# Five small moves in the order of a one-core transformer block: row loads, zeros, turned pair rows, a weight load and late sums

## The chip, the core and the metric

The kernel runs on one core of one Trainium2 chip. The metric is the device time of one execution in microseconds. The core has a matrix engine (TensorE, "PE", with its weight loads "PEld"), VectorE ("DVE"), ScalarE ("ACT"), GpSimd ("POOL") and SyncE ("SP"), which run side by side and wait for each other by semaphores. Each executes its own instructions in order. Transfers (DMAs) are issued by SP, ACT and POOL.

## What is computed

Eight sequences (batches) of 512 rows of 256 numbers go through an attention layer and a mixture of experts, each normalized before and after and added to its input:

```python
x = L0_attn_x
x = x + _layernorm(_L0_attn_ref(_layernorm(x, axis=-1), ...), axis=-1)
x = x + _layernorm(_L0_ffn_ref(_layernorm(x, axis=-1), ...), axis=-1)
```

The attention has 16 query heads of 128 over 4 groups of keys and values, with sinusoidal positions added to queries and keys, and is causal:

```python
scores = jnp.einsum('bgqtd,bgksd->bgqts', q, k) / math.sqrt(D)
scores = jnp.where(causal, scores, -jnp.inf)
probs = jax.nn.softmax(scores, axis=-1)
out = jnp.einsum('bgqts,bgksd->btgqd', probs, v).reshape(b, t, G * QPG * D)
return out @ wo
```

The second layer sends each row to the best 6 of 64 experts by a softmax over gate scores. An expert takes at most 64 rows, the first in the order of rows; what it takes more of counts as zero. A shared expert is added for all rows:

```python
g = jax.nn.silu(jnp.einsum('ech,ehf->ecf', buf, w_gate))
u = jnp.einsum('ech,ehf->ecf', buf, w_up)
d = jnp.einsum('ecf,efh->ech', g * u, w_down)
...
y = y + gs * us @ sh_down.T
```

## The kernel before

**Steps.** The main loop (lines 998 to 1061) runs over 128 steps, one for each head of each batch: step k is head s = k mod 16 of batch b = k // 16. A step holds the scores of head k (`scores`, L328: four blocks of rows `psc`, 0 to 3, each reduced by VectorE with the mask, L332, and put through the exponential by ScalarE, L335), the weighting of the last results (`weigh`: a reciprocal on VectorE, L342, and four multiplications on POOL, L345), the output projection of head k-3 (`project`, L402), the queries of head k+1 (`queries`, L315 and L318) and the product of probabilities and values of head k-2 (`mix`, L390). The order of instructions on all engines is written by hand: what stands first in the Python program stands first in each engine's queue.

**Turned blocks.** For `mix` the probabilities must be transposed. `turned` does so for head k-1 in step k, between the scores of rows 1 and 2: VectorE transposes 32x32 blocks into `eb` (L361), SP writes them to DRAM in four pieces (`ex_d`, L366) and reads them back in the other order as `et` (L371). Rows of a batch that are needed transposed take the same way (`exchange_rows`): four writes to `exr_d` (L133), and a read (L135) that waits in a list and is issued by the next `turned` between its writes and its read of `et`. In this way the next batch's normalized rows become `xr_a`, and the rows of the second layer become `xt2` ("xt" in the profile) for batches 0 to 3.

**Work beside the heads.** `side(s, place)` calls what is planned for a place of a step: A after `weigh`, B after `project`, M after `queries`, D after `mix`. There the second layer of batch b-1 runs in the steps of batch b (`feed_forward`): sums, norms and residuals, the turn of its rows (6M), the shared expert (psg and psu of L749 from step 8 for batches 0 to 3, whose steps from 7 on stand one later, else from 7), the routing, and for batches up to 4 the store of rows and scores into a table in DRAM. `prepare(b+1)` is the other side chain: it loads the next x (L167, called in step 6 before `queries`), takes its norms at the end of step 7 (L78, `st_a`), turns its rows in step 9 and makes keys and values. x has two buffers. `zeros` (L228) writes zeros into the second half of `y_d`, in 21 pieces of 128x256 after a first call; in batch 0 each step asks for two of them, after `mix` (L1034).

**Expert pairs.** The rows of batches 0 to 4 (EARLY = 5) go through 32 pairs of experts (`experts`, L662). One advance of this generator is half of a pair's turn m. In the first half stand the gather of pair m's rows by POOL (`start_pair`, gx, three buffers), then `down` of pair m-5 (pd, L616), `gate_up` of m-3 (pgu, L590), `turn_hidden` of m-4 (pth, L607, and the copy ht), `turn_rows` of m-2 (two transposes ptx, L579, VectorE's copy gxt and the copy gw of two columns, L583), and the weight loads of pairs m-1 (wgu) and m-3 (wd), issued by ACT. In the second half stand `gate_up_hidden` of m-3 (two VectorE instructions, L599 and L600) and the scattering sum by POOL (`scatter`, L627) of m-5. From step 98 on a step has four slots: after the scores of rows 1, after `project`, after `mix` and at its end; first halves fall on the second and fourth, second halves on the first and third. psc, ptx and pth all take their PSUM buffers in turn from `ps_s`, which has three.

**The late pair.** Rows of batches 5 to 7 that still find room in an expert go through one pair, "late", whose number is computed. At step FIRST_FREE = 102, SP loads its weights (`load_gate_up` with 704 KB and `load_down` with 352 KB, L1044 and L1045); they are first used at steps 107 and 109. The next x, for batch 7, is loaded at the end of the same step.

**Early outputs.** After the last pair (step 115) two slots a step, after `queries` and at the end, serve `finish_early` (L969), which finishes batches 0 to 4 (`finish`, L699, and `output`, L686). Each batch begins four slots after the one before it: ACT loads its two halves of y from `y_d` (L703), SP its residual rows x1 one slot later (L716); VectorE adds the halves one slot later (L707); then come the sums for the norm (L78, with POOL's power, L88), and in the next slot `shifts` on VectorE (L94), the scaling on ACT (L98) and the sum with x1 on POOL (L694); two slots later SP stores. `output` also serves batches 5 and 6.

```python
            for _ in range((0, 0, 0, 0, 0, 0, 1, 0, 1, 1, 2, 1, 1, 1, 2, 1)[s] if b == EARLY + 1 else 0 if b > EARLY else
                           (0, 0, 0, 0, 0, 0, 0, 1, 0, 0, 1, 1, 2, 1, 2, 2)[s]):
                next(ahead)()
```

These lines give the places of the rest of `prepare`.

Of the kernel before, what the change touches and what calls it, by code (L numbers as in the profile page):

```python
# [11 lines left out]
F32 = mybir.dt.float32  # L12
# [4 lines left out]
ALU = mybir.AluOpType  # L17
AX = mybir.AxisListType

P = 128  # L20
B, T, E = 8, 512, 256
NT = B * T
NI = T // P
# [5 lines left out]
NH = G * QPG  # L29
NX, F, TOPK, CAP = 64, 176, 6, 64  # L30
FC = F // 2
NM = NX // 2
# [7 lines left out]
EARLY = 5  # L40
# [4 lines left out]
def sandwich_kernel(ctx, tc, x, wq, bq_t, wkv, bk_t, bv, wo, gate_wt, w_gate, w_up, w_down,  # L45
                    sh_gate_t, sh_up_t, sh_down_t, pe_t, out):
    nc = tc.nc
# [4 lines left out]
    small = ctx.enter_context(tc.tile_pool(name="small", bufs=4))  # L52
# [20 lines left out]
    def norm_scales(tiles, name):  # L73

        n = len(tiles)
        st = small.tile([P, n, 6], F32, tag="st", name=f"st_{name}")
        for i in range(n):
            nc.vector.bn_stats(st[:, i, :], tiles[i])  # L78
        return scales_of(st, n, name)
# [11 lines left out]
    def shifts(mv, rs, name):  # L91

        shift = small.tile([P, NI], F32, tag="shift", name=f"shift_{name}")
        nc.vector.scalar_tensor_tensor(shift, mv[:, :, 0], -1.0, rs, ALU.mult, ALU.mult)  # L94
        return shift
# [4 lines left out]
    def tiles_of(t):  # L100
        return [t[:, i, :] for i in range(NI)]
# [44 lines left out]
    with ExitStack() as part:  # L146
# [411 lines left out]
        def load_gate_up(key):  # L558
            l, queue = pairs[key], nc.sync if key == "late" else nc.scalar
            m = l["m"]  # L560

            l["wgu"] = p3.tile([P, 2, 2, 2, F], F32, name=f"wgu_{key}", **l.get("wgu_at", {"tag": "wgu"}))
            for k, w in enumerate((w_gate, w_up)):
                queue.dma_start(out=l["wgu"][:, :, k, :, :].rearrange("p e c f -> p e (c f)"),
                                in_=w[ds(m * 2, 2)].rearrange("e (p c) f -> p e (c f)", p=P))

        def load_down(key):
            l, queue = pairs[key], nc.sync if key == "late" else nc.scalar
            m = l["m"]
            l["wd"] = p3.tile([FC, 2, 2, E], F32, name=f"wd_{key}", **l.get("wd_at", {"tag": "wd"}))  # L570
            queue.dma_start(out=l["wd"].rearrange("p e c h -> p e (c h)"),
                            in_=w_down[ds(m * 2, 2)].rearrange("e (p c) h -> p e (c h)", p=FC))
# [53 lines left out]
        def scatter(m):  # L626
            nc.gpsimd.indirect_dma_start(  # L627
                out=y_d[:, :], out_offset=bass.IndirectOffsetOnAxis(ap=table["idx"][:, m, 1:2], axis=0),
                in_=pairs.pop(m)["dd"], in_offset=None, compute_op=ALU.add)
# [32 lines left out]
        def experts():  # L662


            yield from tables()
            yield
            later = free_slots()
            for m in range(NM + 5):
                if m < NM:
                    start_pair(m)  # L670
                for behind_, step in ((5, down), (3, gate_up), (4, turn_hidden), (2, turn_rows),
                                      (1, load_gate_up), (3, load_down)):
                    if 0 <= m - behind_ < NM:
                        step(m - behind_)
                yield
                if 0 <= m - 3 < NM:
                    gate_up_hidden(m - 3)
                if 0 <= m - 5 < NM:
                    scatter(m - 5)
                if m >= 2:  # L680
                    next(later, None)
                if m == NM + 4:
                    pairs["all"] = True
                yield

        def output(b, y, x1):  # L686

            mv, rs = norm_scales(tiles_of(y), f"y{b}")
            yield
            shift = shifts(mv, rs, f"y{b}")  # L690
            for i in range(NI):
                scale_on_act(y[:, i, :], y[:, i, :], rs, shift, i)
            for i in range(NI):
                nc.gpsimd.tensor_add(x1[:, i, :], x1[:, i, :], y[:, i, :])  # L694
            yield
            nc.sync.dma_start(out=rows_of(out, b * T), in_=x1)
            yield

        def finish(b, tags):  # L699

            ys = [q.tile([P, NI, E], F32, tag=tag, name=f"y{n}_{b}") for n, (q, tag) in enumerate(tags[:2])]
            for k in range(2):
                nc.scalar.dma_start(out=ys[k], in_=rows_of(y_d, k * (ET_ROWS + CAP) + b * T))  # L703
            yield
            x1 = residual(b, *tags[2])
            yield
            nc.vector.tensor_add(ys[0], ys[0], ys[1])  # L707
            yield
            for n, _ in enumerate(output(b, ys[0], x1)):
                yield  # L710
                if n == 1:
                    yield

        def residual(b, q, tag):
            x1 = q.tile([P, NI, E], F32, tag=tag, name=f"x1_{b}")
            nc.sync.dma_start(out=x1, in_=rows_of(x1_d, b * T))  # L716
            return x1
# [251 lines left out]
        def finish_early():  # L969
            rows = [finish(b, EARLY_TAGS + [[(p1, "xn"), (p2, "xnt")][b % 2]]) for b in range(EARLY)]  # L970
            yield

            for t in range(4 * EARLY + 3):
                for b in range(EARLY):
                    if 0 <= t - 4 * b < 7:
                        next(rows[b])
                yield

# [8 lines left out]
        behind, ahead = {}, iter(())  # L987
        routed, zeroing = experts(), zeros()
        twice, finishing = False, False
        FIRST_FREE = (EARLY + 1) * NH + 6  # L990

        def side(s, place):
            behind.pop(f"{s}{place}", lambda: None)()
            if not b:
                for u in rest.get(f"{s}{place}", ()):
                    u()

        for k in range(NK):
            b, s = divmod(k, NH)
            active = k >= EARLY * NH + 14  # L1000
            scores(k, 0)
            scores(k, 1)
            if 0 <= k - 1 < NK - 2:
                turned(k - 1)
            if twice and not finishing:
                next(routed, None)
            scores(k, 2)
            scores(k, 3)
            if k == NK - 1:
                turned_at_once(k - 1)  # L1010
            weigh(k)
            side(s, "A")
            if k >= 3:
                project(k - 3)
            side(s, "B")
            if active and not finishing:
                next(routed, None)
            if s == 9 and b <= EARLY + 1:
                next(ahead)()
            if s == 6 and b <= EARLY:  # L1020
                ahead = prepare(b + 1)
                next(ahead)()
            if k + 1 < NK:
                queries(k + 1)
            if finishing:
                next(routed, None)
            side(s, "M")
            if b <= EARLY and s == 8:
                next(ahead)()
            if k >= 2:  # L1030
                mix(k - 2)
            if active and not finishing:
                next(routed, None)
            if not b:  # L1034
                next(zeroing, None)
                next(zeroing, None)
            if k == FIRST_FREE:

                work = table["work"]
                table["rest"] = nc.values_load(work[0:1, 0:1], min_val=0, max_val=NM - 1)  # L1040
                table["m"] = nc.values_load(work[0:1, 1:2], (ET.DVE, ET.SP), min_val=0, max_val=NM - 1)
                pairs["late"] = {"m": table["m"], "wgu_at": {"tag": "wgu_late", "bufs": 1},
                                 "wd_at": {"tag": "wd_late", "bufs": 1}}
                load_gate_up("late")  # L1044
                load_down("late")  # L1045
            if s == 2 and b:
                behind = feed_forward(b - 1)
            side(s, "D")
            if s == 6 and b == EARLY + 1:
                ahead = prepare(b + 1)  # L1050
# [4 lines that stand above are left out]
            twice = active and k > EARLY * NH + NH  # L1055
            if twice and not finishing:
                next(routed, None)
            if finishing:
                next(routed, None)
            if active and not finishing and "all" in pairs:  # L1060
                routed, finishing = finish_early(), True
# [11 lines left out]
        with tc.For_i(0, table["rest"], 1) as n:  # L1073
            m = nc.values_load(table["work"][0:1, ds(n + 2, 1)], (ET.DVE, ET.SP), min_val=0, max_val=NM - 1)
# [77 lines left out]
```

## Time and profile before

| | |
|---|---|
| median of three runs | 1431.27 us (1430.13 to 1436.82) |
| the profiled execution | 1429.28 us, of which the span is 1427.6 us |
| granted TensorE clock over the span | 0.994 |
| transfers | 262.50 MB, 184 GB/s in the mean |
| VectorE, ScalarE, GpSimd busy | 895.4, 500.2 and 433.7 us |

The profile is of one execution. In a row of groups stand the line, the engine, the operation with what it writes and reads, the count, the busy time with the mean of one instruction in ns, and after the last bar the idle time before them with what ended it. A plain step takes 7.76 us of TensorE. The costliest groups around the change are these:

```profile
L345 POOL TENSOR_SCALAR e<-e,recip 128x128 f32<-128x128 f32 x508 | 268.5, 574 | 757.6 <-DVE recip L342 744.0
L361 DVE STREAM_TRANSPOSE eb<-e 128x128 f32<-128x128 f32 x756 | 227.4, 364 | 3.5 <-DMA ex_d<-eb 3.2
L627 POOL DMA_INDIRECT y_d<-dd,idx x32 | 50.9, 1591 | 102.0 <-DMA y_d<-dd,idx 51.5
```

The transfers by the line that issues them:

```profile
ex_d<-eb SPq DMA_DIRECT2D x504, 160.0 KB
et<-ex_d SPq DMA_DIRECT2D x126, 640.0 KB
wgu<-in_w_gate ACTq DMA_DIRECT2D x32, 352.0 KB
wgu<-in_w_up ACTq DMA_DIRECT2D x32, 352.0 KB
wd<-in_w_down ACTq DMA_DIRECT2D x32, 352.0 KB
y<-y_d ACTq DMA_DIRECT2D x10, 512.0 KB
x<-in_x SPq DMA_DIRECT2D x8, 512.0 KB
```

### The profile page before, as it was taken

Reading aid. Unit: us, or ns where it says so; the run is one execution under the profiler, and the core shown is the slowest. Engines: PE = TensorE matmul, PEld = TensorE weight load, DVE = VectorE, ACT = ScalarE, POOL = GpSimd, SP = SyncE. Lnnn points to the kernel's source line nnn. Section 1 sums busy time; section 2 is a strip of 40 time slices with the busy share of each in tenths; the row PEclk is TensorE's granted clock in tenths of the full one; section 3 lists DMA queues with packets and bytes.
Section 4 is the critical chain, followed back from the end, with each engine's and each line's share of the span. In section 5 each row is a group of like instructions: output and inputs, shape, how many; then the busy total and the mean of one; then the engine's idle time right before and its main releaser. Section 6 shows DMA issues by size and latency. Waiting matters only on the chain.

```text
span 1427.6 us, 18526 instructions
## 1 busy us (share of the span) xinstructions
PE 1383.4 (97%) x5230; PEld 841.4 (59%) x5230; DVE 895.4 (63%) x3127; ACT 500.2 (35%) x1432; POOL 433.7 (30%) x698
## 2 busy tenths in 40 slices
PE   9999999999999999999999999999989999999895
PEld 5665665666556665656556665655546565556463
DVE  5565577656775577557765677566656545677634
ACT  2332344224332334234422433233433333444421
POOL 2222242213321242114221232124545344444311
PEclk9999999999999999999999999999999999999998
DMA  7774566546763576455654566459999889877702
GB/s 243 204 225 146 140 181 198 146 119 171 215 177 107 150 208 193 110 140 164 207 164 125 155 173 193 107 147 276 302 246 258 225 239 252 210 236 250 240 30 82
DMA packets 167990, 262.50 MB, mean 184 GB/s; under 512 B 17212, under 2 KB 142109, under 8 KB 167885
## 3 DMA queue, kind: packets, MB, share of 16 engines
q1 hardware_dynamic: 133069, 212.00, 50.5%
q10 hardware_dynamic: 28672, 39.85, 9.4%
q0 software_dynamic: 6144, 9.44, 3.4%
q8 instruction: 42, 0.69, 0.2%
q14 instruction: 63, 0.52, 0.1%
HBM read 148.25 MB, written 112.99 MB: 183 GB/s over the span
## 4 chain that ended last, share of the span: by engine, by line
PE 80%; DMA 7%; DVE 7%; issue 2%; ACT 2%; POOL 1%; SPq 1%; ACTq 0%; DVEq 0%; POOLq 0%
PE pav L390 16%; PE psc L328 15%; PE pq L315 13%; PE po L402 13%; PE pk L285 4%; PE pv L296 4%; PE psg L749 3%; PE psu L749 3%; PE pgu L590 2%; PE py L776 2%; PE pd L616 2%; DMA wd<-in_w_down 2%; DVE eb L361 1%; DMA exr_d<-xb_f 1%; ACT e L335 1%
## 5 line engine op out<-in xcount | busy, mean ns | idle before, releaser
L345 POOL TENSOR_SCALAR e<-e,recip 128x128 f32<-128x128 f32 x508 | 268.5, 574 | 757.6 <-DVE recip L342 744.0
L335 ACT ACTIVATE e<-e,least 128x128 f32<-128x128 f32 (+3 forms) x512 | 285.8, 559 | 349.2 <-DVE least L332 337.1
L328 PE MATMUL psc<-kt,qt 128*128 128x128 f32 (+3 forms) x1024 | 306.3, 438 | 8.6 <-DVE least L332 6.0
L390 PE MATMUL pav<-et,v 128*128 128x512 f32 (+3 forms) x1024 | 297.5, 434 | 3.3 <-DMA et<-ex_d 3.0
L390 PEld LDWEIGHTS pav<-et,v 128*128 128x128 f32 x1024 | 194.1, 190 | 165.7 <-issue 116.8
L332 DVE CUSTOM_DVE_ANT_0 e<-psc,mask 128x128 f32<-128x128 f32 (+3 forms) x512 | 232.6, 479 | 56.3 <-PE psc L328 49.4
L402 PE MATMUL po<-wo_sb,ao 128*128 128x256 f32 x1024 | 243.5, 381 | 0.7 <-ACT ao L110 0.7
L315 PE MATMUL pq<-xnt,wq_sb 128*128 128x512 f32 x512 | 242.2, 596 | 0.0
L402 PEld LDWEIGHTS po<-wo_sb,ao 128*128 128x128 f32 x1024 | 193.1, 190 | 72.0 <-issue 41.0
L110 ACT COPY ao<-pav 128x512 f32<-128x512 f32 x128 | 74.9, 585 | 443.8 <-PE pav L390 429.6
L361 DVE STREAM_TRANSPOSE eb<-e 128x128 f32<-128x128 f32 x756 | 227.4, 364 | 3.5 <-DMA ex_d<-eb 3.2
L328 PEld LDWEIGHTS psc<-kt,qt 128*128 128x128 f32 x1024 | 164.6, 191 | 76.7 <-DVE least L332 26.9
L318 DVE SCALAR_TENSOR_TENSOR qt<-pq,bq_sb,pe_sb 128x512 f32<-128x512 f32 x128 | 95.6, 747 | 104.6 <-PE pq L315 104.4
L315 PEld LDWEIGHTS pq<-xnt,wq_sb 128*128 128x128 f32 x512 | 96.3, 191 | 69.7 <-issue 64.3
L342 DVE RECIPROCAL recip<-total 128x4 f32<-128x4 f32 x128 | 22.8, 178 | 120.2 <-ACT e L335 120.2
L335 ACT ACTIVATION_READ_ACCUMULATOR e<-e,least 128x1 f32 x512 | 95.8, 187 | 0.0
L627 POOL DMA_INDIRECT y_d<-dd,idx x32 | 50.9, 1591 | 102.0 <-DMA y_d<-dd,idx 51.5
L285 PE MATMUL pk<-xnt,wkv_sb 128*128 128x512 f32 x128 | 59.3, 594 | 0.2 <-ACT xnt L110 0.2
L296 PE MATMUL pv<-wkv_sb,xnt 128*128 128x512 f32 x128 | 58.1, 593 | 0.0
L298 DVE TENSOR_TENSOR v<-pv,bv_sb 128x512 f32<-128x512 f32 x32 | 22.1, 691 | 49.7 <-PE pv L296 49.7
L288 DVE SCALAR_TENSOR_TENSOR kt<-pk,bk_sb,pe_sb 128x512 f32<-128x512 f32 x32 | 24.0, 750 | 44.1 <-PE pk L285 44.1
L113 DVE COPY ht<-pth 88x256 f32<-88x256 f32 x32 | 13.4, 418 | 56.6 <-PE pth L607 56.6
(200 smaller groups left out, 1100.0 us busy)
## 6 DMA issues: line engine op xcount, KB each, us to landing
ex_d<-eb SPq DMA_DIRECT2D x504, 160.0 KB
et<-ex_d SPq DMA_DIRECT2D x126, 640.0 KB
wgu<-in_w_gate ACTq DMA_DIRECT2D x32, 352.0 KB
wgu<-in_w_up ACTq DMA_DIRECT2D x32, 352.0 KB
wd<-in_w_down ACTq DMA_DIRECT2D x32, 352.0 KB
y<-y_d ACTq DMA_DIRECT2D x10, 512.0 KB
x<-in_x SPq DMA_DIRECT2D x8, 512.0 KB
x_d<-x SPq DMA_DIRECT2D x8, 512.0 KB
```

The source lines that it names most:

```text
L285: nc.tensor.matmul(pk, lhsT=wkv_sb[:, c, g, 0, :], rhs=s["xnt"][:, c, :], start=c == 0, stop=c == NC - 1)
L296: nc.tensor.matmul(pv, lhsT=s["xnt"][:, c, ts(i, P)], rhs=wkv_sb[:, c, :, 1, :], start=c == 0, stop=c == NC - 1)
L315: nc.tensor.matmul(pq, lhsT=wq_sb[h // QPG][:, c, ts(h % QPG, D)], rhs=seqs[b]["xnt"][:, c, :], start=c == 0, stop=c == NC - 1)
L318: nc.vector.scalar_tensor_tensor(qt, pq, bq_sb[:, h : h + 1], pe_sb, ALU.add, ALU.add)
L328: nc.tensor.matmul(psc[:, :w], lhsT=l["qt"][:, ts(i, P)], rhs=seqs[b]["kt"][h // QPG][:, :w], start=True, stop=True)
L332: nc.vector.tensor_tensor_reduce(out=e, in0=psc[:, :w], in1=mask[:, T - w :], scale=-1.0 / math.sqrt(D), scalar=BIG, op0=ALU.add, op1=ALU. ...
L335: nc.scalar.activation(e, e, AF.Exp, bias=l["least"][:, i : i + 1], scale=-1.0, accum_out=l["total"][:, i : i + 1])
L345: engine.tensor_scalar(e, e, recip[:, n : n + 1], 1.0, ALU.mult, ALU.mult)
L361: nc.vector.transpose(blocks.rearrange("p c j t -> p j c t"), l["e"][i][:, js[0] * P : (js[-1] + 1) * P].rearrange("p (j c t) -> p j c t", ...
L390: nc.tensor.matmul(pav[:, :, j:, :], lhsT=seqs[b]["v"][:, j, ts(g, D)], rhs=l["et"][:, :, AT[j] : AT[j] + NI - j, :], start=j == 0, stop=j ...
L402: nc.tensor.matmul(po[b][i // 2][:, i % 2, :], lhsT=ao[:, ts(i, P)], rhs=wo_sb[:, h, :], start=h == 0 and i % 2 == 0, stop=h == NH - 1, sk ...
L749: nc.tensor.matmul(as_taken(pp[:mw, :], xt2), lhsT=w_sb[:, c, ds(f0, mw)], rhs=in_order(xt2, c), start=c == 0, stop=c == NC - 1)
```

## The change

Nothing that is computed changes. Six things move.

- `zeros` is asked for one piece a step instead of two, through the first 23 steps, so that the last pieces fall into batch 1.
- In step 6 the load of the next x stands after `queries` and place M instead of before `queries`. For batches 1 to 4 place M of this step issues the writes to `exr_d`.
- `turn_rows` of pair m-2 moves from the first half of the turn to the end of the second half, behind `scatter`.
- `load_down("late")` is issued at step 104 instead of 102.
- The two halves of an early y are added on GpSimd, in the slot in which x1 is loaded, which stands three slots after the loads of y instead of one. The sums for the norm follow two slots later. A batch so takes nine slots instead of seven, and the last two of all fall into `last_part`.
- `output` makes the shift of two instructions, a multiplication by -1 on VectorE before the slot ends and a product with the power on GpSimd, instead of one on VectorE in the next slot.

```diff
-                for behind_, step in ((5, down), (3, gate_up), (4, turn_hidden), (2, turn_rows),
-                                      (1, load_gate_up), (3, load_down)):
+                for behind_, step in ((5, down), (3, gate_up), (4, turn_hidden), (1, load_gate_up), (3, load_down)):
...
                 if 0 <= m - 5 < NM:
                     scatter(m - 5)
+                if 0 <= m - 2 < NM:
+                    turn_rows(m - 2)
...
             mv, rs = norm_scales(tiles_of(y), f"y{b}")
-            yield
-            shift = shifts(mv, rs, f"y{b}")
+            shift = small.tile([P, NI], F32, tag="shift", name=f"shift_y{b}")
+            nc.vector.tensor_scalar_mul(shift, mv[:, :, 0], -1.0)
+            nc.gpsimd.tensor_tensor(shift, shift, rs, ALU.mult)
+            yield
...
             yield
+            yield
+            yield
             x1 = residual(b, *tags[2])
-            yield
-            nc.vector.tensor_add(ys[0], ys[0], ys[1])
+            nc.gpsimd.tensor_add(ys[0], ys[0], ys[1])
+            yield
             yield
...
-            for t in range(4 * EARLY + 3):
+            for t in range(4 * EARLY + 5):
                 for b in range(EARLY):
-                    if 0 <= t - 4 * b < 7:
+                    if 0 <= t - 4 * b < 9:
...
-            if s == 6 and b <= EARLY:
-                ahead = prepare(b + 1)
-                next(ahead)()
             if k + 1 < NK:
                 queries(k + 1)
             if finishing:
                 next(routed, None)
             side(s, "M")
+            if s == 6 and b <= EARLY:
+                ahead = prepare(b + 1)
+                next(ahead)()
...
-            if not b:
-                next(zeroing, None)
+            if k < NH + 7:
                 next(zeroing, None)
...
                 load_gate_up("late")
+            if k == FIRST_FREE + 2:
                 load_down("late")
```

## The prediction

> **What bounds the kernel now.** A "step" is one head k = 16b + s. I read the busy shares first, then TensorE's waits, then the clock and transfers by stage, and then the chain and the timelines around each wait. Times are of the profiled execution: span 1427.6 us, device time 1429.3, which is 2.0 below the median of 1431.3.
>
> ```profile
> PE 1383.4 (97%) x5230; PEld 841.4 (59%) x5230; DVE 895.4 (63%) x3127; ACT 500.2 (35%) x1432; POOL 433.7 (30%) x698
> ```
>
> TensorE is busy 97% of the span and the diff removes no matmul. So the change can win only out of the 44 us in which TensorE idles (1427.6 - 1383.4), and out of time in which it runs at half clock. Who TensorE waits for:
>
> ```profile
> PE psc L328 <- DVE least L332: 6.0, 6, 2.4
> PE psg L749 <- DMA xt<-exr_d: 4.7, 4, 1.5
> PE pav L390 <- DMA et<-ex_d: 3.0, 3, 2.3
> PE pd L616 <- DMA wd<-in_w_down: 2.9, 2, 2.1
> PE ptx L579 <- DMA gx<-xg_d,idx: 2.3, 1, 2.3
> PE pe L380 <- ACT et L110: 2.2, 1, 2.2
> ```
>
> The columns are total us, times, longest. These are 21 us, and each part of the change lies beside one of them. The stages (pairs begin; pairs run; weights for "late" arrive; later pairs):
>
> ```profile
> 942.60:972.50 29.90, 27.63 (x101) 16.66 (x100) 16.52 (x65) 9.89 (x30) 10.31 (x16) 0.94 0.63 191
> 972.50:1028.30 55.80, 55.49 (x279) 32.72 (x278) 39.57 (x149) 21.66 (x61) 28.52 (x34) 1.00 0.97 287
> 1028.30:1065.30 37.00, 33.46 (x151) 18.72 (x150) 20.11 (x70) 13.96 (x41) 14.63 (x16) 0.95 0.96 259
> 1065.30:1245.20 179.90, 178.68 (x847) 103.50 (x845) 100.63 (x332) 65.02 (x173) 80.98 (x89) 1.00 0.86 239
> ```
>
> After the busy times come the granted clock, the DMA share and GB/s. The clock falls only in the two stages that hold the gx and wd waits, and the transfers are full (0.96, 0.97) from 972 to 1065.
>
> **1. Zeros by single pieces.** At step 11 TensorE waits 2.3 us for et. On SP's queue two zero writes (1.46 us of issuing, 256 KB) stand between the writes of the turned batch rows and the ex_d writes, whose eb is already there; et, issued at 106.3, lands 6.4 us later. One piece less: half of the 1.46 us, 0.7, and half a microsecond of transfer. The other pieces go to steps 11 to 21, where the DMA share is 0.5 to 0.7 and TensorE waits for nothing. Between 0 and 2.8 (with the half microsecond lost at step 8): I take **1.5**.
>
> **2. Next x behind the exr_d writes** (batches 1 to 4, step 6).
>
> ```profile
> 215.07 0.40 SPq L167 DMA_DIRECT2D x<-in_x  x1
> 215.56 2.48 SPq L133 DMA_DIRECT2D exr_d<-xb_f  x4
> 218.09 2.80 SPq L366 DMA_DIRECT2D ex_d<-eb  x4
> 222.13 0.34 SPq L135 DMA_DIRECT2D xt<-exr_d  x1
> ```
>
> The 512 KB of x go ahead of the four writes. These land 4.72 us after the last issue (the chain), and xt another 3.68 after its own, at 225.81, when psg has waited 1.47. With the writes first, xt should start 1.5 to 2 us earlier and all 4.7 us of the four waits could go. The price is x itself: it lands about 1.4 us later (at 222.0 instead of 220.6, the same bytes in the other order). VectorE takes its sums (st_a) at 220.87 in front of step 8's reductions, and the fourth psc of that step already starts only when the first reduction ends. With the sums begun at 222.0 instead of 220.9, the reduction behind them ends at 224.0; psc could go on at 223.46. So some 0.55 us per batch come back as a wait of psc. 4.7 - 4 x 0.55 = **2.5**; ends -1 (x later still) and 4.7.
>
> **3. Pairs' rows turned half a pair later.** The first gather:
>
> ```profile
> 958.53 6.21 DMA gx<-xg_d,idx
> 964.74 0.14 issue
> 964.88 0.48 PE ptx L579 x2
> 965.35 3.08 PE pq L315 x4
> 968.44 2.49 PE pav L390 x8
> ```
>
> The new place is behind pq and pav of that step, 1.7 + 2.2 us of TensorE work from 962.6, so 966.5; the gather lands at 964.7. The 2.27 us go. So does the half clock after them: four pq take 3.08 instead of 1.72 and pav 2.49 instead of 2.16, 1.7 us. The Trainium skill (TensorE: Matmul & The Clock Gate, "What's actually happening") puts the fall to half rate after an idle window of about 3.4 us. By that rule a 2.3 us wait costs no clock and the part is worth 2.3; the row shows 0.94 in this stage, so I count 4.0. Against it, the first pair's gate_up then follows its ptx directly and waits for the copy (0.4 us and its semaphores): -0.7. **3.3**.
>
> In the other pairs the rotation of ps_s's three buffers changes. Now psc 1 of a step takes the buffer of pth, issued just before, and waits for its copy: DVE ht ends at 1000.33 and psc goes on at 1000.37, 0.2 us late. After the change ptx lies between them. 17 steps x 0.2 = 3.4. Against it, in every second slot gate_up comes 0.93 us (pd) after its ptx. VectorE's hid instructions end before pd begins in all of these slots but one (1012.0 against 1010.9), so I charge 0.4 us. POOL's next gather waits for gw, but weigh stands ahead of that gather or long after it; nothing. The copies (0.41 + 0.35) now delay the reductions of scores 2 and 3 by 0.8 us, covered by the 3 us between POOL's weigh and the next transposes. If DVE's queue is later than I read it, this turns round: -3 to 3.9. I take **2.0**.
>
> **4. wd_late two steps later.** At 1028 to 1031 SP issues 704 KB, 352 KB and x's 512 KB within 3 us; the wd load of 1028.85 takes 14.76 us and that of 1044.10 takes 9.30 (the chain). Without 352 of the 1568 KB the burst is 1.25 us shorter (at 280 KB/us). The first wait (0.84) goes and the second (2.10) shrinks, with perhaps its 1.7 us of half clock. But the bytes return at about 1056, where the share is still near 0.9. Between -1 and 4.6: **2.0**.
>
> **5. Early sums on GpSimd, more slots, shift on two engines.**
>
> ```profile
> 1323.98 1.23 DVE L707 TENSOR_TENSOR y<-y,y 128x1024 f32<-128x1024 f32 x1 [5.11 <-DMA ex_d<-eb]
> 1325.12 0.28 DVE L332 CUSTOM_DVE_ANT_0 e<-psc,mask 128x128 f32<-128x128 f32 x1
> ```
>
> VectorE stands 5.1 us in front of this add (y landed only at 1322.0), the reductions stand behind it, and TensorE waits 2.40. From 1245 on such waits of psc are 5.2 us in five, at 1262 (an add, 0.5), 1292 (sums, 1.3), 1323 (2.4), 1334 and 1352 (shift waits for POOL's power of 1.02 us; 0.3 and 0.7). The add leaves VectorE's queue, shift's first half needs no POOL, and the y loads get one more slot before the add and two before the sums. The sums move from even s to odd: the collision at s = 8 goes, one with the routing at s = 9 comes (sums 1.9 + routing 1.3 against about 2.4 of slack: 0.8).
>
> Two pages of the skill speak against it. GPSIMD Engine Reference, "Engine selection", gives elementwise adds to VectorE, GpSimd being about twice as slow. The trace agrees: POOL's 128x256 adds take 729 ns, so 128x1024 some 2.9 us (an estimate from L694) against 1.22. By engine time the part costs 5 x 1.7 = 8.4 us; but POOL is busy for 46 of 105 us here, and behind the add stands only the next step's weigh, some 8 us later. SBUF - State Buffer, "Who interferes with whom", says that a VectorE copy or tensor_scalar in its two-port mode is shut out by a GpSimd instruction for its whole length. The trace shows it: L107's four take 1.84 us beside POOL's four L345 of 2.21. By the rule at its worst each add stops VectorE for 2.9 us, 14.6 in all. But reductions and transposes keep their times beside POOL's adds, and only the routing at s = 8 has such instructions then: 0.7. 5.2 - 0.8 - 0.7 = **3.7**; ends 0 and 5.5.
>
> In step 127 ScalarE scales batch 4's y for 2.08 us in front of the last exponentials and the et copies for which TensorE waits 2.2. The scaling now comes behind mix of 125, beside 7.8 us of matmuls. 1.3 of the 2.2 could go; the sums join VectorE's tail. **1.0**, ends -1 and 2.2.
>
> **Sum.** 1.5 + 2.5 + 3.3 + 2.0 + 2.0 + 3.7 + 1.0 = 16.0. 1429.3 - 16.0 = 1413.3, and 1415.3 beside the median: **1415**.
>
> **Rivals.**
> (a) Transfers, not TensorE, set the stage from 972 to 1065 (share 0.97): then what part 3 frees is waited for at wd, and the moved bytes only move the wait. Parts 3 and 4 give nothing, the others 8.7: 1429.3 - 8.7 + 2.0 = 1422.6, at the edge of what can be told from no change. Against it: only 2.9 us of waits for wd stand in that stage. 0.14.
> (b) The slower side: gxt late. ptx, pd and gate_up are now one chain in every second slot and in the other ptx stands behind six transposes. If VectorE reaches the copy 0.5 us after pd begins, gate_up stalls. All else (16.0 without the 2.0 of the rotation) gives 14.0, so it decides from 14.0 / 32 = 0.44 us per pair on; at 0.75 us (a copy of 0.41 and the 0.35 of gw ahead of the next pair's) it costs 24: 1431.3 + 24 - 14 = 1441. Against it are the ends of hid above. 0.10.
> (c) The adds lock VectorE: part 5 is -9.4 instead of 3.7 (5.2 - 14.6): 1428. 0.06.
> The forecast has 0.70.
>
> **Numbers.** 0.5% (7 us, about what a measurement can tell from no change) puts faster below 1424.1 and slower above 1438.4. Forecast nearly all faster, (a) a half, (c) a quarter: 0.75; slower nearly all of (b): 0.09; the rest 0.16. All parts at their good ends give 27.7 and 1404; I leave out that corner, and most of (b): 1407 to 1430.
>
> **What would show it.** Right: no wait of ptx for gx and clock 1.00 in that stage; psg's waits gone, psc's reappearing at step 8 of batches 1 to 4 at about 0.5; one short wait of pav at step 11; psc's waits for reductions after 1245 below 2 us; TensorE's busy time unchanged. Wrong: pgu waiting for gxt, longer wd waits, ACT or SP held at loads, or VectorE's tensor_scalars stretched to 3 us beside L711.

## The result, and the profile after

1424.53 us median (1423.25 to 1427.62, 8 runs) against 1431.44 for the kernel before on the same chip: ratio 0.9959, 95% interval 0.9945 to 0.9974. That is 6.9 us less; 16.0 were forecast. A second series, run with the experiments, gave 1425.12 (1423.79 to 1429.15) against 1430.59, ratio 0.9961 [0.9945, 0.9976]. The direction was right and the time lies in the range, but less than half of the gain came.

The profiled execution took 1423.79 us, its span 1422.1. The busy row, and the view of waits (total us, times, longest), of the kernel after:

```profile
PE 1381.5 (97%) x5230; PEld 839.4 (59%) x5230; DVE 889.2 (63%) x3122; ACT 499.4 (35%) x1432; POOL 446.1 (31%) x710
```

```profile
PE psc L328 <- DVE least L332: 9.9, 8, 2.5
PE pav L390 <- DMA et<-ex_d: 3.7, 3, 1.7
PE ptx L579 <- DVE ht L113: 2.8, 1, 2.8
PE pt_f L120 <- DVE xg L107: 2.0, 5, 1.1
...
PE psg L754 <- DMA xt<-exr_d: 0.4, 1, 0.4
...
PE pd L616 <- DMA wd<-in_w_down: 0.3, 1, 0.3
```

Of the six waits shown of before, psg's for xt fell from 4.7 to 0.4, pd's for wd from 2.9 to 0.3, and ptx's for gx and pe's for et left the list. In this profile each of those parts did remove its wait. But psc's waits for reductions grew from 6.0 to 9.9 us, and ptx waits 2.8 us for something new. Steps tell where (from the first psc of a step to that of the next or, for the last, to the start of the last matmul):

| steps | before | after |
|---|---|---|
| 8 to 15 (zeros) | 78.93 | 76.56 |
| step 8 of batches 1 to 4 (x behind the writes) | 50.46 | 51.92 |
| 98 to 115 (pairs, wd_late) | 286.64 | 278.84 |
| 116 to 126 (late outputs) | 104.57 | 110.93 |
| 127 and the end's matmuls | 62.04 | 59.12 |

The row of steps 116 to 126 looks like the culprit: 6.4 us longer. It was not, mostly: a profile is one execution. Over the profiles made here these steps take 105.8 us in the mean of four without part 5 and 107.8 in nine with it, and the experiments below undo the part and time it.

### The profile page after: what moved, and what is told of

It reads as the page before. It is cut to its first block, busy times and chain, and to the rows that moved or that the text cites. A ratio compares the mean times of both kernels' runs of the same rounds, so it can differ in the third digit from the quotient of the medians.

```text
span 1422.1 us, 18484 instructions
## 1 busy us (share of the span) xinstructions
PE 1381.5 (97%) x5230; PEld 839.4 (59%) x5230; DVE 889.2 (63%) x3122; ACT 499.4 (35%) x1432; POOL 446.1 (31%) x710
## 4 chain that ended last, share of the span: by engine, by line
PE 83%; DMA 6%; DVE 6%; ACT 1%; issue 1%; POOL 1%; SPq 1%; ACTq 0%; DVEq 0%; POOLq 0%
PE pav L390 17%; PE psc L328 16%; PE po L402 13%; PE pq L315 13%; PE pk L285 4%; PE pv L296 4%; PE psg L754 3%; PE psu L754 3%; PE pgu L590 2%; PE py L781 2%; PE pd L616 2%; DMA ex_d<-eb 1%; DMA et<-ex_d 1%; DMA x<-in_x 1%; DMA y<-y_d 1%; DVE eb L361 1%
## 5 line engine op out<-in xcount | busy, mean ns | idle before, releaser
L590 PE MATMUL pgu<-wgu,gxt 128*64 128x352 f32 x256 | 43.6, 461 | 1.0 <-issue 0.8
```

## The experiments

All times are medians, with the ratio to the kernel before on the same chip. "After" is taken at 1424.8, the middle of its two series.

**One part undone at a time.** First the late outputs (`output`, `finish` and the slots as before), then the x load (put back ahead of `queries`):

```diff
+            if s == 6 and b <= EARLY:
+                ahead = prepare(b + 1)
+                next(ahead)()
             if k + 1 < NK:
                 queries(k + 1)
...
             side(s, "M")
-            if s == 6 and b <= EARLY:
-                ahead = prepare(b + 1)
-                next(ahead)()
```

> Only part 5 is undone (output, finish and the slots as before; the sums y added by VectorE again). If part 5 itself lost the 6.4 us that steps 116 to 126 grew by, these steps go back from 110.9 us to about 104.6 and the tail from step 127 from 74.8 to about 77.8: 1421 in all, 3.4 less than after. If the loss came from the other parts (the stage is reached 8.9 us earlier, so other transfers meet it), the steps stay near 111 and the tail's 3 us are lost: 1427 to 1428.

> Only part 2 is undone (the x load stands ahead of queries and the exr_d writes again). If x landing later costs VectorE's sums, and with them the reductions of step 8, more than the psg waits were worth: step 8 of batches 1 to 4 goes back from 51.9 to 50.5 us in all, the psg waits return (4.7 us) and the psc waits there fall below 1 us in all: 1423, 1.5 less than after. If part 2 is worth what was predicted of it, and the psc waits have another cause: 1427.

Without part 5: 1429.13, ratio 0.9997 [0.9982, 1.0012]. Undoing the part that seemed to lose 6.4 us lost another 4.3. Without part 2: 1419.78, ratio 0.9931 [0.9906, 0.9956], 5.0 us **faster** than after (4.1 by the two ratios); all its six executions (1417.4 to 1422.0) lie below all fourteen of after (1423.3 to 1429.2). So part 2, more than part 5, is where the forecast went wrong. The waits of psg come back in that profile:

```profile
PE psg L754 <- DMA xt<-exr_d: 4.2, 4, 1.7
PE psc L328 <- DVE least L332: 4.0, 3, 2.5
```

Step 8 of batches 1 to 4 took 50.3 us there. Over all the profiles made here it takes 49.6 to 50.5 in the five with before's order of x (mean 50.2), and 51.9 to 56.5 in the nine with after's (mean 54.0).

Then part 3 (turn_rows back in the first half of the pair) and part 4 (wd_late back beside wgu_late), with the changed kernel once more:

> The changed kernel once more, beside the next three on the same chip: 1424 to 1425. In its profile step 8 of batches 1 to 4 takes 52 to 56 us, as in the three other profiles that have part 2, against 50.3 and 50.5 in the two that have it not.

> Only part 3 is undone (the pairs' rows are turned in the first half of the pair again). By the prediction the wait for gx of 2.3 us at step 98 and its half clock return and the 2.0 us of the rotation are lost: steps 98 to 115 grow by about 5 us, 1430. If the new wait of ptx for ht at step 105 (2.8, 1.3, 2.0, 1.2 and 3.3 us in the five profiles with part 3) belongs to part 3, it goes, and only some 3 us are lost: 1427 to 1428.

> Only part 4 is undone (wd_late loaded together with wgu_late again). By the prediction 2.0 us are lost: 1426.5, and the waits of pd for wd at steps 103 and 104 are back at 2 to 3 us. If the burst of loads is long enough without it, or part 3 alone has shifted the pairs, the waits stay below 1 us and the time at 1424 to 1425.

After: step 8 of batches 1 to 4 took 54.8. Without part 3: 1426.52, ratio 0.9975 [0.9965, 0.9986], a loss of 1.7, less than either theory had, and its interval overlaps most of after's. Without part 4: 1427.92, ratio 0.9983 [0.9971, 0.9995], a loss of 3.1. The wait for ht stays in the profile without part 3, only on another instruction (psc, 2.0 us), so it does not belong to that part; and without part 4 no wait for wd came back in the profiled execution (pq waited 2.1 us for ScalarE's sc there), so that the median, not the profile, speaks for part 4.

**Why part 2 lost.** SyncE's queue in batch 2 before (the prediction shows batch 1), with TensorE's wait; start, length, what:

```profile
371.28 0.40 SPq L167 DMA_DIRECT2D x<-in_x  x1
371.85 2.19 SPq L133 DMA_DIRECT2D exr_d<-xb_f  x4
374.10 3.01 SPq L366 DMA_DIRECT2D ex_d<-eb  x4
378.10 0.34 SPq L135 DMA_DIRECT2D xt<-exr_d  x1
```

```profile
381.84 1.52 PE L749 MATMUL psg<-xt,sg_sb 128*128 128x512 f32 x3 [0.89 <-DMA xt<-exr_d]
```

And the kernel after, batch 1, first its queue, then VectorE and TensorE:

```profile
212.82 1.76 SPq L133 DMA_DIRECT2D exr_d<-xb_f  x4
214.63 0.49 SPq L167 DMA_DIRECT2D x<-in_x  x1
215.17 2.99 SPq L366 DMA_DIRECT2D ex_d<-eb  x4
218.61 0.34 SPq L135 DMA_DIRECT2D xt<-exr_d  x1
...
220.61 1.41 DVE L78 BATCH_NORM_STATS2 st_a<-x 128x6 f32<-128x256 f32 x4 [2.21 <-DMA x<-in_x]
...
222.40 0.28 DVE L332 CUSTOM_DVE_ANT_0 e<-psc,mask 128x128 f32<-128x128 f32 x1
...
222.75 1.12 PE L328 MATMUL psc<-kt,qt 128*128 128x512 f32 x2 [1.68 <-DVE least L332]
```

Measured from the start of step 8, the exr_d writes begin at -6.78 us in both kernels (batch 1 of before alone: -6.59). They wait for xb_f (in batch 1 of after its last transpose ends at 212.80, and the writes begin at 212.82), and the x load ahead of them had been issued while the queue had nothing else to do. Behind the writes, x lands 0.1 to 1.0 us after step 8 begins; before, st_a ran at -1.3 without waiting. Now VectorE stands 2.2 us for x, its sums take 1.8 us, and step 8's first reduction starts 2.8 us into the step instead of 0.5. The fourth psc waits 1.68 us (0.81, 1.20, 1.60 in batches 2 to 4).

That leaves the question whether xt at least came earlier. So the sums were moved behind step 8's reductions:

```diff
             side(s, "A")
+            if b <= EARLY and s == 8:
+                next(ahead)()
...
-                           (0, 0, 0, 0, 0, 0, 0, 1, 0, 0, 1, 1, 2, 1, 2, 2)[s]):
+                           (0, 0, 0, 0, 0, 0, 0, 0, 0, 0, 1, 1, 2, 1, 2, 2)[s]):
```

> After, with one thing moved: the next batch's sums st_a are taken by VectorE behind the reductions of step 8 (behind its weigh) instead of in front of them. If part 2 loses because the later x holds these sums, and with them the reductions of step 8, the psc waits there (5.3 us in batches 1 to 4) fall below 0.3 each while the psg waits stay gone: step 8 of batches 1 to 4 takes about 46 us instead of 52 or more, and the time is 1418 to 1419.5. If the order of the queue itself (x behind the writes) costs something else, the time stays above 1423.

1429.52, ratio 0.9995 [0.9984, 1.0006]: 4.7 us slower than after. The psc waits went, as expected; the psg waits did not stay gone. TensorE in batch 1:

```profile
225.77 1.10 PE L754 MATMUL psg<-xt,sg_sb 128*128 128x512 f32 x2 [1.83 <-DMA xt<-exr_d]
```

In the four batches psg waits 1.83, 2.17, 1.76 and 2.26, more than before. In after these waits had only been covered by those of psc. xt is issued about 0.7 us earlier than before (at -0.8 to -1.2 us from the start of the step instead of -0.0 to -0.6; in after at -1.0 to -1.5), but takes 4.8 to 5.5 us to land instead of 3.6 to 3.9, because the 512 KB of x are now under way beside it: it lands at 4.0 to 4.4 us into the step, before at 3.1 to 3.7. (With the sums moved, psc also waits 2.2 us at step 9 of batch 5, where it was 0.8.)

If that is the cause, xt must land early wherever x is out of its way. First x was issued later still, behind the reads of xt and et in step 7 (the block moved from `s == 6` to `s == 7`, behind `turned(k - 1)`, sums as in the last experiment); then, in another kernel, earlier, at step 3 of batches 1 to 3:

```diff
-            t = p2.tile([P, NI, E], F32, tag="x", name=f"x_{b}")
+            pool_, tag = (p3, "wgu") if b == 2 else (p2, "x")
+            t = pool_.tile([P, NI, E], F32, tag=tag, name=f"x_{b}")
...
-            if s == 6 and b <= EARLY:
+            if s == (3 if b in (1, 2, 3) else 6) and b <= EARLY:
```

> After, with the next x issued still later, behind the reads of xt and et in step 7, and its sums taken behind the reductions of step 8. If xt is late because the 512 KB of x are still in flight when it is read, in either order of the writes, xt now lands some 2 us earlier (about 2 us after step 8 begins instead of 3 to 4.5), the psg waits and the psc waits of step 8 both go: step 8 of batches 1 to 4 takes about 45.5 us instead of 50.4 (without part 2) or 52 to 56 (with it), and the time is 1416 to 1418. If xt is bound by its own writes, psg's waits stay at 0.8 to 2 us each and the time is above 1420; if x is now too late for its sums, step 9 grows beyond its 33.4 us.

> After, but in batches 1 to 3 the next x is loaded at step 3 (x of batch 2 into a buffer that the pairs use only later), so that its 512 KB are out of the burst of step 7; batch 4 as in after. If xt is late because x is in flight beside its writes and reads, xt lands about 2.5 us after step 8 begins, and neither psg nor psc waits there in batches 1 to 3: step 8 takes about 11.4 us in these three and 13.3 in batch 4, 47.5 in all against 54.0 in the mean of nine profiles with part 2 and 50.3 without it: 1418 to 1419. If xt is bound by its own writes and the ex_d traffic, psg still waits 0.7 to 1.5 us in each and the time is 1420 to 1422.

With x behind xt, xt landed 2.4 to 2.65 us into step 8 and psg waited 0.5 us at most. But x itself came 5.8 to 8.6 us into the step; VectorE stood for it in front of gs, and pav waited for gs (1.47, 1.40 and 0.87 us in batches 1 to 3), and psc at step 9 of batch 5 waited 2.2 as in the last experiment: 1428.98, ratio 0.9988 [0.9972, 1.0004], well off the 1416 to 1418 expected. The mechanism held, the forecast of the time did not. With x at step 3: 1421.57, ratio 0.9937 [0.9916, 0.9959], where 1418 to 1419 was expected. Batch 2 there, queue and TensorE:

```profile
372.22 1.97 SPq L133 DMA_DIRECT2D exr_d<-xb_f  x4
374.48 2.37 SPq L367 DMA_DIRECT2D ex_d<-eb  x4
377.02 0.34 SPq L135 DMA_DIRECT2D xt<-exr_d  x1
...
379.00 2.32 PE L329 MATMUL psc<-kt,qt 128*128 128x128 f32 x8
381.20 1.10 PE L755 MATMUL psg<-xt,sg_sb 128*128 128x512 f32 x2
```

No row has idle time in brackets: neither psc nor psg waits. Step 8 took 11.63, 11.31 and 11.19 us in batches 1 to 3 and 13.30 in batch 4, whose x was left as in after: 47.4 in all, 47.5 expected. That is 6.6 us less than the mean of 54.0, of which the median shows 3.2; where the rest went is open. In these three batches xt is issued at -0.8 to -2.1 us and takes 3.2 to 4.0 to land. So xt is late because of x's transfer in either order of issue: ahead of the writes it delays them and with them the issue of xt, behind them it delays the landing of xt. What helps is x away from that place.

**Part 2 alone** on the kernel before:

> The kernel before with part 2 alone. If part 2 costs by itself what its removal from after gave back (4.7 to 5.3 us): 1434 to 1436. If it is worth the 2.5 us of the prediction: 1428. If it costs only where the other parts stand too: 1430 to 1431.

1432.31 against 1430.29, ratio 1.0014 [0.9999, 1.0029]: 2.0 us slower, step 8 of batches 1 to 4 at 54.1. The price is smaller than the 5.0 that undoing it gave back; the steps' 3.8 (54.0 - 50.2) lie between the two.

**The late stage.** What the forecast feared of the sums on GpSimd is there once in an execution. Kernel after at step 121, VectorE, then GpSimd:

```profile
1285.24 0.32 DVE L438 TENSOR_SCALAR xg<-sc,grecip 128x64 f32<-128x64 f32 x1
1285.59 0.23 DVE L439 MAX8 top<-xg 128x8 f32<-128x64 f32 x1
1285.74 2.13 DVE L438 TENSOR_SCALAR xg<-sc,grecip 128x64 f32<-128x64 f32 x1
```

```profile
1285.47 2.35 POOL L711 TENSOR_TENSOR y<-y,y 128x1024 f32<-128x1024 f32 x1
```

An instruction of 0.24 us takes 2.13, until GpSimd's add ends; the reductions behind it are late and psc waits 2.5. Three variants of part 5 were tried: the add on VectorE, the add on GpSimd in four pieces of 128x256, and the x1 load one slot earlier (in after it goes out together with the next batch's y loads and an out write, 2 MB, and pav then waits 1.6 us for et).

```diff
-            nc.gpsimd.tensor_add(ys[0], ys[0], ys[1])
+            for i in range(NI):
+                nc.gpsimd.tensor_add(ys[0][:, i, :], ys[0][:, i, :], ys[1][:, i, :])
```

> After, but the early sums are added by VectorE again, in after's slots. If GpSimd's add shuts VectorE out (L438 took 2.13 us beside it at step 121), the psc wait of 2.52 us at step 121 and the half clock behind it (1.7 us) go, and each add costs VectorE 1.23 us in other places, of which perhaps 1 us in all is waited for: steps 116 to 126 take about 107.5 us, 1421. If the late stage is slow by its transfers (the y loads, the x1 load and the out write of three batches in one burst), nothing but the place of the wait changes: 1424 to 1425, and the pav waits of 1.6 and 1.7 us stay.

> After, with each early sum on GpSimd done in four pieces of 128x256. If GpSimd's 2.35 us instruction shuts VectorE's L438 out for its whole length at step 121, a piece (0.7 us) does so for less: the psc wait of 2.52 us there falls to about 1 us, steps 116 to 126 take some 1.5 us less (without the half clock behind that wait 3), 1422 to 1423.5. If VectorE's instruction stays shut out between the pieces too, the wait stays at 2.5 and the time at 1425.

> After, but each x1 load is issued one slot earlier, so that it no longer goes out together with the next batch's y loads and an out write (2 MB in one burst). If that burst makes et late, the pav waits of 1.64 and 1.67 us at steps 124 and 126 shrink below 0.5 each: 1421.5 to 1422.5. If GpSimd's add, and not the burst, is the cause of the late stage's loss, they stay and the time stays at 1424 to 1425.

VectorE adding: 1423.94, ratio 0.9956 [0.9941, 0.9971]; psc at step 121 waits 1.3 instead of 2.5, the pav waits stay at 1.8 and 1.6. Four pieces: 1422.66, ratio 0.9955 [0.9938, 0.9971]; VectorE's L438 now take 0.5 us each and psc waits 1.4. x1 earlier: 1423.61, ratio 0.9957 [0.9944, 0.997]; one pav wait of 0.6 is left of the two. Each made its own wait smaller, as expected, and none moved the ratio by more than its interval; the 1421 and the 1421.5 to 1422.5 expected of the first and the third did not come. Which engine adds hardly matters.

Part 5, and parts 3 and 4, alone on the kernel before:

> The kernel before with part 5 alone. Undoing part 5 in after lost 4.2 us by the medians, while the mean of its last twelve steps over the profiles is only 0.8 us shorter with it. If part 5 is worth what the medians say: 1426 to 1427 against 1430.4. If the profiles' steps are right: 1429 to 1430.

> The kernel before with parts 3 and 4 alone. Undone one by one in after they lost 1.6 and 3.0 us; steps 98 to 115 are 5.4 us shorter in the mean of ten profiles that have both; the prediction has 7.3. If the measured ones add up: 1425 to 1426. If the prediction's sizes hold outside after: 1423. If the wait of ptx for ht at step 105 eats them where the stage is reached at another time: 1428.

Part 5: 1426.82, ratio 0.9975 [0.9962, 0.9987], 3.9 us. Parts 3 and 4: 1425.21, ratio 0.9962 [0.9948, 0.9976], 5.5 us.

**A better kernel.** Without part 2, with the pieces and the earlier x1; then the same with the early x:

> After without part 2, with the sum on GpSimd in four pieces and each x1 load one slot earlier. If the three effects add up: 1419.8 less about 1.5 for the pieces and 1 to 2 for the pav waits: 1416 to 1418. If the late stage's waits only change places, as they did with the sums on VectorE, 1419 to 1421.

> The same early x in batches 1 to 3, the x load of the other batches ahead of the queries as before, the early sums in four pieces and each x1 load one slot earlier. If the effects add up: 1419.4 (measured without the early x) less 3 x 1 us of psg waits: 1416 to 1417. If not: 1419 to 1420.

1419.38, ratio 0.9926 [0.99, 0.9952], no better than leaving out part 2 alone. With x at step 3 in batches 1 to 3: **1415.47**, ratio 0.9899 [0.9872, 0.9926], faster than both kernels; psg's waits there are 2.0 us in all.

## Why the prediction was off, point by point

| part | predicted | by steps of the profiles | by runs |
|---|---|---|---|
| 1 zeros | 1.5 | 1.8 (steps 8 to 15: 79.4 in 4 without, 77.6 in 12 with; the two with the sums moved left out) | not run alone |
| 2 x behind the writes | 2.5 | -3.8 | -2.0 [-4.1, 0.1] alone; -5.0 in after |
| 3 and 4 pairs, wd_late | 7.3 | 5.3 (steps 98 to 115: 284.8 in 3, 279.5 in 13) | 5.5 [3.4, 7.4] alone; 1.7 and 3.1 in after |
| 5 and the last step | 4.7 | 0.8 (steps 116 to 127: 167.7 in 4, 166.9 in 9) | 3.9 [1.9, 5.4] alone; 4.3 in after |

**Part 2 is the step that failed**, with the wrong sign (clear of noise where it was taken out of after, just not where it was run alone): "With the writes first, xt should start 1.5 to 2 us earlier and all 4.7 us of the four waits could go." The writes did not start earlier: xb_f, not x, was what they waited for. What x costs is its transfer beside theirs and xt's, in either order of issue, and not a place in the queue. Where its landing can be read (the sums moved), xt was issued 0.7 us earlier in the mean and landed 0.4 to 1.3 us later than before. The second term, "some 0.55 us per batch come back as a wait of psc", had the right mechanism at less than half its size (1.3 in the mean of the four): x landed at 0.1 to 1.0 us into the step, where the working had -0.2 (222.0 against a start of 222.16). The low end of that part's range, -1, was too high as well. Between +2.5 and -3.8, the reading by steps, lie 6.3 of the 9.1 us by which the gain fell short (4.5 by the run of part 2 alone, 7.5 by taking it out). Rival (a) had the right kind of reason, moved bytes that only move a wait, at the wrong place.

**Parts 3 and 4** removed the wait for gx in all profiles, and brought that for wd to 0.75 us or less in all but one of the 13 with both parts (1.8 us in the kernel with VectorE adding). The stage of the gx wait, where the prediction shows a clock of 0.94, in the kernel after:

```profile
933.67:963.50 29.83, 29.83 (x105) 18.08 (x104) 19.46 (x77) 10.41 (x31) 9.06 (x16) 1.00 0.58 164
```

The mean lengths of the steps in three profiles without both parts and in the 13 with both tell where 7.3 became 5.3:

| steps | predicted | gained |
|---|---|---|
| 98 (wait for gx, half clock, pgu's wait) | 3.3 | 4.2 |
| 99 to 102 and 106 to 115 (rotation of the buffers) | 2.0 | 0.2 |
| 103 and 104 (waits for wd) | 2.0 | 3.3 |
| 105 (ht) | 0 | -2.3 |

The waits were worth more than was counted. The rotation was mis-sized: steps 99 to 102 lose 1.0, the later ones gain 1.1. And VectorE was late next: at step 105 ht's copy stands behind the routing and the sums st_a, and ptx waits 1.2 to 3.3 us for it in all 13 profiles, a term that the sum did not have. How the 5.3 divides between the two parts is open: without part 3, steps 98 to 115 of the one profile took 285.1 us against 279.5, but the median lost only 1.7. Rival (b), gxt late pair after pair, did not come; gate_up's waits for gxt are at most 0.6 us, two or three times in the execution.

**Part 5** was about right by the runs. The lock at step 121 was priced at 0.7 us; psc waits 2.5 there, and 1.3 with VectorE adding. The waits of pav for et were not foreseen; on the other side the last step gained 2.9 where 1.0 was counted. psc's waits for reductions after 1245, forecast below 2, are 3.2, from 5.2. The steps of single profiles show only 0.8 us for the whole part; the two readings do not agree within what I can explain, and the size is left open between them. Rival (c), five locks, fell: one of the five adds meets a tensor_scalar of VectorE.

**Part 1** agrees by the steps, and pav's wait at step 11 is 1.7 to 2.3 us in the four profiles without it, 0.4 to 2.0 in the others. The runs do not show it: the other parts alone already add to 7.4 us, more than the whole change gained, with intervals of about 2 us to either side.

The chances: faster by over 0.5% had 0.75. By the median, 6.9 us or 0.48%, the change ends just inside "within 0.5%".

## What to carry to other kernels

Before a transfer is moved out of another's way in a queue, look at what the second one waits for when the queue reaches it: if its data were not ready, the first costs it no place in the queue, only bytes in flight, and moving it back puts these bytes beside the next, more urgent transfer. Here only moving it well away from both helped. When a wait vanishes in the new profile, test whether its cause is gone or merely covered by an earlier wait; moving the coverer away tells. And where executions scatter by several us, a stage of one profile cannot be blamed: undo the part and time it.

## What the runs showed of the hardware

**Half clock comes by fixed windows.** Every stretch of half clock within a kernel is 3.41 us long or a multiple, and within one execution they begin whole multiples of 3.41 us apart. Laid out on that grid, every window in which TensorE was busy for less than 0.45 of the time was followed by a half-clock one, 47 windows in 18 profiles, 18 of them at the end of the kernel (the start-up is left out). From 0.454 on this came only three times after windows in which most of the work was transposes (0.54 to 0.60, at pt_f; another of that kind, 0.50, did not fall), and once after a window that ran at half clock itself. Windows of the kernel after, then of its second profile; after the length come the busy times of TensorE, its weight loads, VectorE, ScalarE and GpSimd; the third number from the end is the granted clock:

```profile
1055.60:1059.01 3.41, 0.68 (x5) 0.27 (x3) 3.27 (x17) 0.00 (x0) 1.60 (x2) 1.00 1.03 274
1057.31:1060.72 3.41, 1.68 (x6) 1.11 (x7) 3.38 (x18) 0.99 (x4) 0.06 (x1) 1.00 0.99 299
1286.01:1289.42 3.41, 0.89 (x4) 0.27 (x3) 3.31 (x9) 0.28 (x2) 1.81 (x1) 1.00 0.92 280
1289.42:1292.83 3.41, 3.41 (x7) 2.02 (x7) 2.88 (x12) 1.87 (x7) 0.00 (x0) 0.50 0.98 310
```

```profile
222.27:225.68 3.41, 1.48 (x4) 0.62 (x4) 3.38 (x17) 0.99 (x4) 1.02 (x1) 1.00 0.78 225
225.68:229.09 3.41, 3.41 (x5) 1.35 (x4) 1.98 (x8) 1.82 (x5) 0.39 (x2) 0.50 0.83 256
693.31:696.72 3.41, 1.58 (x8) 0.92 (x8) 2.29 (x12) 0.72 (x2) 0.35 (x1) 1.00 0.87 324
696.72:700.13 3.41, 3.41 (x9) 1.45 (x10) 2.90 (x12) 1.87 (x7) 0.67 (x1) 1.00 0.79 240
```

The last four rows show the border: 1.48 us busy (0.43) fell, 1.58 (0.46) did not.

The wait of 2.5 us at step 121 left 0.89 of one grid window busy (0.26), and the next ran at half. The longer wait of 2.8 us at step 105 left only 0.68 us of the first stretch busy, but that stretch is not on the grid; on it the wait is shared between two windows, the second of them 1.68 busy (0.49), and the clock stayed. The section of the Trainium skill that the prediction used (TensorE: Matmul & The Clock Gate, "What's actually happening") also says that the window is free-running and 3413 ns long. The grid here agrees with that, and the working left it out; that the window before a fall is an idle one does not hold here, since more than 0.4 of it may be busy. Within the 128 steps, apart from those at pt_f, each fall had a single wait of 1.9 to 3.3 us before it. So a wait of that length costs another 1.7 us (half of 3.41) or nothing, by where it falls. The profiles held from none to five such stretches between start and end; the two of the kernel after had two (1423.79 us) and four (1429.15). Time and mean granted clock go together: over the 42 executions of the kernel before on the chip of the first experiments their correlation is -0.72, about half of the variance. The 4.0 that the prediction counted for the wait for gx (2.3 to 2.8 us) stood: in all four profiles without part 3 the clock fell after it.

**One tensor_scalar of VectorE is held until a GpSimd add ends**, not all those beside it: one of 2.13 us instead of 0.24, then three at 0.24. With the add in four pieces three of them take 0.5 each. GpSimd needs 2.34 to 2.36 us for 128x1024 in four of the five adds and 2.79 in one, against the 2.9 estimated from pieces.
